# A four-layer metaformer on one core: the ranking's end reordered with rows from a root, and layer 1's normed rows on ScalarE

## The chip, the cores and the metric

The kernel runs on one core of a Trainium2 chip, in one launch. The metric is device time in microseconds (us), the median of several runs; a profile of one more execution shows what each engine did. The engines are TensorE (PE; its weight loads are shown as PEld), VectorE (DVE), ScalarE (ACT), GpSimd (POOL) and SyncE (SP), which here issues DMAs. Each engine works through its own queue in order.

## The reference

The input is an image batch x of shape (4, 64, 128, 128), fp32, seen as 256 matrices of 128 rows ("tokens") by 128 channels. Four layers follow one another, each with two residual halves: x + mixer(norm(x)), then x + ffn(norm(x)). The change lies in layer 1 (the second one):

```
# mixer of layer 1, per matrix (n = 128 rows)
score  = -(|q_i|^2 + |k_j|^2 - 2 q_i.k_j)        # 128 x 128, q = k = centred rows
ranks  = argsort(argsort(-score)) + 1            # place of each entry among all 128*128
weight = -log(ranks / (128*128));  weight /= sum over each row
x = x + dec(weight @ enc(norm(x)))
# ffn of layer 1
p, i = top_k(softmax(norm(x) @ router_w + router_b), 2);  p /= sum(p)
x = x + sum_k p_k * (norm(x) @ expert_w[i_k] + expert_b[i_k])      # 8 experts
```

Equal scores are ranked in order of their place in the matrix, since argsort is stable.

## The kernel before

The layers run one after another. Layer 1 is built of `l1_distances` (norm, products, the distances of all pairs), `l1_ranks` (the ranking) and `l1_blocks` (weights, values, experts).

**Ranking.** The 256 matrices are two groups of 128, one matrix on each partition. The distance matrix is symmetric, so only the upper triangle is sorted: 8128 pairs, padded to 8192 numbers per partition. `sort_stage` runs a merging network forward and stores which pairs were exchanged; `back_stage` runs it backwards on the places, so that `ranks[g]` holds each pair's rank, with flags for equal neighbours. Its end is `finish(g, ta, tb)`, called for group 0 and then for group 1:

- ScalarE copies the ranks to fp32 (L1546), VectorE finds the largest eight of each segment of 256 (L1550, L1551), which are the equal ones.
- VectorE masks the ranks (L1553), ScalarE spreads them into two halves of an int32 (L1556, two instructions), SyncE writes them to DRAM, one DMA for each of 127 rows of the triangle (L1560).
- The candidates are packed and up to 64 per partition picked (L1567 to L1584). Each is a place f in the triangle; its row is the number of row ends that are not above f: a comparison of 64 x 128 (L1591) and a sum (L1596). From row and column come two positions per equal pair, and a comparison of 128 x 128 (L1615) with a sum (L1620) tells how many come before each. TensorE turns the results (L1628), ScalarE keeps them in `ties` (L1629).

This part is ordered by a scheduler that works from the program's dependencies. A branch (L1835), at which all engines meet, chooses a slow path that is not taken with this input. Behind it come the constants of `l1_blocks` and its loads of the written ranks.

**Blocks.** `l1_blocks` handles eight matrices at a time, in 32 blocks. Each step is given to a planner (`Plan`) with its engine, an assumed time, what it reads and what it writes; the planner then fixes one order per engine over all blocks, in which several blocks overlap, so a change of a step's engine or assumed time can change the whole order. A block loads xt and the ranks (rt); GpSimd casts these to `above` and `below` (L2213). `normed` is run twice per block, ahead of the attention (k = "1") and ahead of the experts (k = "2"): statistics (`bn`, L1937), their merging (`merge`, L1943 to L1948), a first guess of 1/sqrt by ScalarE (L1952, L1953), its refinement (L1959 to L1963), then the normed rows: of every four, rows 0 and 2 by VectorE (L1979) and rows 1 and 3 by ScalarE (L1977). TensorE turns four of them (L1991, tile pt, two buffers) and ScalarE copies them out (L2003). Attention: `ta` and `tb` mark the equal pairs (L2013, L2014), TensorE adds the ranks up (L2018 to L2022), ScalarE takes the logarithm (L2027), values are made (L2032, L2038), weights times values (L2044), divided and added to x (L2052, L2055). Experts: logits (L2072, L2079), the top two and their shares (L2091 to L2125), turned (L2142) and copied (L2148); for each of eight experts TensorE spreads its share over the partitions (L2156, tile pr, two buffers), the rows are multiplied by it (L2166: five by VectorE, three by GpSimd from ScalarE's copy, L2162), TensorE adds up the products (L2183, L2185) and VectorE adds them to x (L2190). GpSimd stores xt (L2227).

## Time and profile before

| | us |
|---|---|
| runs | 11910.42, 11881.41, 11887.56 (median 11887.56) |
| profiled execution | 11887.27, its span 11885.4 |
| VectorE busy | 10015.2 (84% of the span) |
| ScalarE busy | 7406.1 (62%) |
| TensorE busy | 7219.7 (61%) |
| GpSimd busy | 6180.0 (52%) |
| first instruction behind the branch L1835 on VectorE | at 5277.49 |
| one block of the blocks' stage, L2142 to L2142 | 5838.96 to 5874.38 |

Starts are counted from the span's start. A row of the timeline gives start, duration, engine, line, operation, the tile written and those read, and in brackets the idle time of the engine before it with what ended it. Neighbouring instructions of one kind are merged (x4) and may overlap a little, so the distance between starts can be shorter than a duration. "SPq" is SyncE's queue of DMA issues.

### The profile page before, as it was taken

The numbers are of one execution on the slowest core, as the hardware profiler recorded it, in microseconds if no ns is written. First come the engines' busy times: TensorE is split into PE (matmuls) and PEld (weight loads), VectorE is DVE, ScalarE is ACT, GpSimd is POOL, SyncE is SP. The second block draws the span as 40 slices with busy tenths as digits, with TensorE's granted clock in tenths as the row PEclk, the third lists the DMA queues.
The fourth block names the chain that finished last, engine by engine and source line by source line (L and its number), as shares of the span: only waits on it lengthen the run. The fifth ranks groups of instructions, "written<-read, shape, count | busy, mean of one in ns | idle before, by whom it ended". The sixth has DMA issues, their size and how long they took to land. (4 is left out here: it accounts for less than half of the span.)

```text
span 11885.4 us, 113599 instructions
## 1 busy us (share of the span) xinstructions
PE 7219.7 (61%) x33966; PEld 4411.3 (37%) x33966; DVE 10015.2 (84%) x16358; ACT 7406.1 (62%) x10575; POOL 6180.0 (52%) x5274
## 2 busy tenths in 40 slices
PE   7877785000000000019997899989999999998665
PEld 5655553000000000018886344444444444446443
DVE  7567637999999999988996899999999999997454
ACT  4244534888867777623332787877878787875332
POOL 1000026999960000003232999988999999994222
PEclk8877797555555555559998999999999999999887
DMA  5312245111111111121111334333343433333434
GB/s 191 95 41 49 81 139 136 56 58 58 58 54 55 57 55 54 49 47 45 44 47 32 138 141 143 139 133 139 137 142 137 144 139 141 137 134 116 173 133 152
DMA packets 636713, 1193.45 MB, mean 100 GB/s; under 512 B 217036, under 2 KB 434478, under 8 KB 556974
## 3 DMA queue, kind: packets, MB, share of 16 engines
q1 hardware_dynamic: 592158, 1059.80, 26.6%
q0 software_dynamic: 34368, 124.14, 3.2%
q8 instruction: 273, 4.47, 0.2%
q10 hardware_dynamic: 9552, 2.08, 0.1%
q14 instruction: 362, 2.97, 0.1%
HBM read 950.89 MB, written 251.71 MB: 101 GB/s over the span
## 5 line engine op out<-in xcount | busy, mean ns | idle before, releaser
L2719 POOL TENSOR_TENSOR gs<-hist,cc 128x512 f32<-128x512 f32 x2048 | 2576.0, 1266 | 376.7 <-DVE hist L2714 232.1
L2714 DVE TENSOR_TENSOR_SCAN hist<-da,state,bs 128x512 f32<-128x512 f32 x1984 | 2521.7, 1271 | 0.0
L2728 PE MATMUL py<-gs,ident 128*128 128x512 f32 x4096 | 2241.5, 630 | 5.2 <-DVE y L2604 5.2
L1628 PE MATMUL pt<-ident,both 128*128 128x128 f32 x6 | 2.7, 447 | 3257.1 <-DMA pk<-spare 3185.5
L2685 ACT ACTIVATE da<-dt,am 128x512 f32<-128x512 f32 x2048 | 1414.6, 715 | 328.9 <-DVE hist L2714 326.6
L2706 DVE TENSOR_TENSOR bs<-dx,bs 128x512 f32<-128x512 f32 x2048 | 1391.3, 679 | 183.5 <-PE bs L2692 138.3
L1504 POOL TENSOR_TENSOR diff<-key 128x2048 f32<-128x2048 f32 (+11 forms) x364 | 1383.8, 3853 | 86.4 <-DVE key L1509 76.4
L1628 PEld LDWEIGHTS pt<-ident,both 128*128 128x128 f32 x6 | 1.1, 182 | 3258.6 <-issue 3258.6
L2728 PEld LDWEIGHTS py<-gs,ident 128*128 128x128 f32 x4096 | 738.0, 197 | 906.0 <-issue 437.3
L1886 POOL IOTA row<- 72x1 int32 x1 | 0.1, 137 | 1799.5 <-ACTq L1835 1799.5
L2692 PE MATMUL bs<-bt,pick 96*128 96x512 bf16 x2048 | 805.8, 394 | 144.5 <-DVE hist L2714 141.4
L1526 ACT COPY keep<-rank 128x1536 int16<-128x1536 int16 (+11 forms) x364 | 612.8, 1686 | 437.5 <-DVE rank L1528 388.6
L1502 ACT COPY low<-key 128x2048 f32<-128x2048 f32 (+11 forms) x364 | 627.4, 1724 | 284.1 <-DVE key L1509 275.7
L1527 DVE COPY_PREDICATED rank<-back,rank 128x1536 int16<-128x1536 uint8 (+11 forms) x364 | 781.4, 2147 | 16.7 <-ACT keep L1526 16.7
L1528 DVE COPY_PREDICATED rank<-back,keep 128x1536 int16<-128x1536 uint8 (+11 forms) x364 | 777.7, 2137 | 12.5
L1509 DVE TENSOR_TENSOR key<-low,key 128x2048 f32<-128x2048 f32 (+11 forms) x364 | 744.3, 2045 | 12.4
L1508 DVE TENSOR_TENSOR key<-low,key 128x2048 f32<-128x2048 f32 (+11 forms) x364 | 748.9, 2057 | 6.4 <-DMA key<-dist 3.9
L1505 ACT ACTIVATE turned<-diff 128x2048 int8<-128x2048 f32 (+11 forms) x364 | 600.2, 1697 | 36.6 <-DMA key<-dist 28.0
L1517 ACT ACTIVATE back<-turned 128x3072 uint8<-128x3072 int8 (+12 forms) x182 | 582.2, 3199 | 0.0
L2185 PE MATMUL pe<-ew,xg 128*128 128x128 f32 x4096 | 506.7, 277 | 0.0
L2185 PEld LDWEIGHTS pe<-ew,xg 128*128 128x128 f32 x4096 | 490.5, 194 | 4.0
L1026 POOL DMA_DIRECT2D state<-zz x16 | 18.5, 1157 | 855.2 <-DVE zz L1016 615.1
(825 smaller groups left out, 18223.0 us busy)
## 6 DMA issues: line engine op xcount, KB each, us to landing
cc<-cd SPq DMA_DIRECT2D x512, 1024.0 KB
xt<-state SPq DMA_DIRECT2D x64, 1024.0 KB
xo<-state SPq DMA_DIRECT2D x128, 256.0 KB
state<-xo POOLq DMA_DIRECT2D x128, 256.0 KB, 2.9
xl<-in_L_ffn_weight SPq DMA_DIRECT2D x32, 1024.0 KB
tk<-in_x SPq DMA_DIRECT2D x32, 512.0 KB
tokens<-tt POOLq DMA_DIRECT2D x32, 512.0 KB, 6.4
pk<-in_l1c_diag SPq DMA_DIRECT2D x32, 512.0 KB
```

The lines of the kernel that those rows point to most:

```text
L1504: nc.gpsimd.tensor_sub(d, lo[part], hi[part])
L1508: nc.vector.tensor_tensor(lo[part], c, hi[part], ALU.min)
L1509: nc.vector.tensor_tensor(hi[part], c, hi[part], ALU.max)
L1527: nc.vector.copy_predicated(l, t, h)
L1528: nc.vector.copy_predicated(h, t, kv)
L2185: T.matmul(w["pe"][:, j, :], w["xg"][:, q, j, :], ew[:, q, :], start=False, stop=(j == 3 and q == E - 1))
L2685: nc.scalar.activation(da, x_["dt%d" % b], AF.Exp, scale=am[:, s : s + 1])
L2692: nc.tensor.matmul(bs, pick[:, s, :], x_["bt%d" % b], start=True, stop=True)
L2706: nc.vector.tensor_mul(db, x_["dx%d" % b], db)
L2714: nc.vector.tensor_tensor_scan(h, live.pop(("da", t)), live.pop(("db", t)), 0.0 if first else state[b][:, s : s + 1], ALU.mult, ALU.add,)
L2719: nc.gpsimd.tensor_tensor(gs, h, live.pop(("cc", t)), ALU.mult)
L2728: nc.tensor.matmul(x_["py%d" % b], env.ident, live.pop(("gs", t)), start=(s == 0), stop=(s == S - 1))
```

## The change

Three things. (1) In `normed`, all eight rows are made by ScalarE, four in one step of an assumed 2.0 us; VectorE's steps of 0.7 and ScalarE's of 1.0 go. (2) In `merge`, the last small operation (variance times 1/C plus eps) is written with eps as a broadcast tensor in place of a scalar from a tile. (3) `finish` is split into `spread`, `candidates`, `equals`, `compare` and `lacking`, called in a new order for the two groups: both copies, group 0's spread, both searches, then the rest. The row of a place f comes from the quadratic's root, by Ln and Exp on ScalarE, and two corrections by at most one row; the comparison with all row ends, its sum and the table of row ends are gone.

```diff
-            nc.vector.tensor_tensor(
-                cmp, f.unsqueeze(2).to_broadcast([P, TIES, W]), rowend.unsqueeze(1).to_broadcast([P, TIES, W]),
-                ALU.is_ge,
-            )
-            nc.vector.tensor_reduce(row, cmp, AX.X, ALU.add)
...
+            nc.vector.tensor_scalar(x, f, -8.0, float((2 * W - 1) ** 2), ALU.mult, ALU.add)
+            nc.vector.tensor_scalar(x, x, 1.0, None, ALU.max)
+            nc.scalar.activation(x, x, AF.Ln)
+            nc.scalar.activation(x, x, AF.Exp, scale=0.5)
+            ri = sb.tile([P, TIES], I32, name="ri")
+            nc.vector.tensor_scalar(ri, x, -0.5, W - 0.5, ALU.mult, ALU.add)
+            nc.vector.tensor_copy(row, ri)
+            def start():
+                nc.vector.tensor_scalar(gap, row, -0.5, W - 0.5, ALU.mult, ALU.add)
+                nc.vector.tensor_mul(gap, gap, row)
+                nc.vector.tensor_sub(gap, f, gap)
+            start()
+            nc.vector.scalar_tensor_tensor(row, gap, 0.0, row, ALU.is_lt, ALU.subtract)
+            nc.vector.tensor_scalar(row, row, -1.0, None, ALU.mult)
+            start()
+            nc.vector.tensor_add(x, gap, row)
+            nc.vector.scalar_tensor_tensor(row, x, W - 1.0, row, ALU.is_ge, ALU.add)
+            start()
...
-        finish(0, keys[0], spare)
-        finish(1, keys[1], spare)
+        for g in range(2):
+            nc.scalar.copy(keys[g], ranks[g])
+        spread(0, spare)
+        found = [candidates(0, keys[0])]
+        found.append(candidates(1, keys[1]))
+        last = [equals(0, *found[0])]
+        before = [compare(last[0][3], keys[0])]
+        spread(1, keys[1])
+        last.append(equals(1, *found[1]))
+        lacking(0, *last[0][:3], before[0])
+        before.append(compare(last[1][3], keys[0]))
+        lacking(1, *last[1][:3], before[1])
...
-                V.tensor_scalar(mv[:, :, 1], mv[:, :, 1], 1.0 / C, eps, ALU.mult, ALU.add)
+                V.scalar_tensor_tensor(mv[:, :, 1], mv[:, :, 1], 1.0 / C, eps.to_broadcast([P, NB]), ALU.mult, ALU.add)
...
+            def affine(j0):
+                def f():
...
+                    for j in range(j0, j0 + 4):
+                        r, n = v["rs"][:, j : j + 1], v["nb"][:, j : j + 1]
+                        S.activation(v["xl"][:, j, :], v["xt"][:, j, :], AF.Identity, bias=n, scale=r)
...
-                    step("dve", 0.7, tags(0) + scales, "xl xl0 " + name, make, new="xl " + name)
+                    step("act", 2.0, tags(0) + scales, "xl xl0 " + name, affine(0), new="xl " + name)
                 else:
-                    step("dve", 0.7, tags(4) + scales + "xl", "xl4", affine((4, 6), V))
-                step("act", 1.0, tags(j0) + scales + "xl", "xm%d" % j0, affine((j0 + 1, j0 + 3), S))
+                    step("act", 2.0, tags(4) + scales + "xl", "xl4", affine(4))
```

`spread` holds the masking, ScalarE's two instructions and the 127 row writes of a group, `candidates` the search by segments, `equals` all from the packing to the positions, `compare` L1615 and `lacking` L1620 and what follows it. Group 1 is spread into `keys[1]`, which its search must have read by then; group 0 into `spare`.

## Prediction

> **What bounds the kernel now.** Views read in this order: the page's span and slices, the stretches of 250 us, the timeline of the ranking's end, SyncE's waits, one block of the blocks' stage engine by engine, and the order in which the two built programs queue their instructions. Only two stretches change order on any engine: the ranking's end (5082 to 5277 us) and layer 1's blocks (5290 to 6473 us). From the page:

> ```profile
> span 11885.4 us, 113599 instructions
> PE   7877785000000000019997899989999999998665
> DVE  7567637999999999988996899999999999997454
> ACT  4244534888867777623332787877878787875332
> ```

> Around slice 18 VectorE is full and TensorE idle; after it both stand at 9. The ranking's end, from its timeline:

> ```profile
> 5123.18 8.69 DVE L1591 TENSOR_TENSOR key<-f,rowend 128x8192 f32<-128x8192 f32 x1
> 5126.68 149.23 SPq L1560 DMA_DIRECT2D pk<-spare  x254
> 5131.99 8.68 DVE L1596 TENSOR_REDUCE row<-key 128x64 f32<-128x8192 f32 x1
> 5194.85 18.69 ACT L1556 ACTIVATE spare<-rank,base 128x8192 int16<-128x8192 int16 x2 [13.30 <-DVE rank L1553]
> 5241.84 17.22 DVE L1620 TENSOR_REDUCE rk<-key 128x128 f32<-128x16384 int16 x1
> 5263.95 0.14 POOL L1886 IOTA row<- 72x1 int32 x1 [1799.52 <-ACTq L1835]
> 5277.49 0.17 DVE L1870 MEMSET rw<- 128x128 f32 x1 [17.38 <-SPq L1835]
> ```

> The 254 row writes are two trains of 127 on SyncE: 5126.7 to 5187.2 (60.5 us) and 5213.6 to 5275.9 (62.3), each after ScalarE's pair of L1556. VectorE ends its last reduction at 5259.06; the branch L1835 lets everybody on at 5277.5, 1.6 us after SyncE's last write. So SyncE ends this stretch, and between its trains it waits for ScalarE, which waits for VectorE. One block:

> ```profile
> 5838.96 0.41 PE L2142 MATMUL pl<-identb,g 128*72 128x128 bf16 x4 [0.44 <-DVE g L2125]
> 5860.99 0.68 PE L1991 MATMUL pt<-ident,xl 128*128 128x128 f32 x4 [0.70 <-DVE xl L1979]
> 5862.23 0.71 PE L1991 MATMUL pt<-ident,xl 128*128 128x128 f32 x4 [0.56 <-DVE xl L1979]
> 5874.38 0.41 PE L2142 MATMUL pl<-identb,g 128*72 128x128 bf16 x4 [0.43 <-DVE g L2125]
> 5851.81 0.53 DVE L1943 TENSOR_TENSOR d<-st 128x8 f32<-128x8 f32 x1
> 5853.60 1.18 DVE L1948 TENSOR_SCALAR mv<-mv,eps 128x8 f32<-128x8 f32 x1
> 5859.77 2.92 DVE L1979 TENSOR_SCALAR xl<-xt,rs,nb 128x128 f32<-128x128 f32 x4
> 5851.28 1.04 POOL L2213 CAST below<-rt 128x1024 f32<-128x1024 int16 x1
> 5853.49 1.27 POOL L2166 TENSOR_TENSOR xg<-xT,gr 128x512 f32<-128x512 f32 x1 [1.17 <-ACT gr L2162]
> 5859.50 2.59 POOL L2166 TENSOR_TENSOR xg<-xT,gr 128x512 f32<-128x512 f32 x2 [4.74 <-ACT gr L2162]
> ```

> Columns: start, duration, engine, line, operation, and in brackets the idle time before and what ended it. A block takes 35.42 us (L2142 to L2142). Pitch is the distance from start to start where nothing waits. TensorE's pitches sum to 31.75: eight L2185 groups of 1.80, four L1991 and two L2072 of 0.89, two L2032 of 0.90, four L2044 of 0.45, two runs L2018 to L2022 of 1.98, 16 L2156 of 0.22, and 0.96 for L2142 and L2183. It loses 0.59 for g (L2142), 0.49 for v and 0.73 for copies in the middle, and 0.87 + 0.79 + 0.10 for normed rows: 3.6. VectorE and GpSimd block each other: L1948 lasts 0.23 alone and 1.18 until GpSimd's product ends; four rows of L1979 last 1.1 alone and 2.9 beside two products.

> **Ranking's end, removed and moved.** L1591 and L1596 go for both groups: 2 x (8.69 + 8.68) = 34.7 us of VectorE. The masking and ScalarE's spread of group 0 come first. ScalarE copies both ranks (7.02 each) until 5089.7, then spreads until 5108.4 (18.7); train 0 starts there, 18.3 us earlier, and ends at 5168.9. Group 1's spread needs its candidates read: 5082.6 + 2.3 (mask) + 2 x 23.05 (64 pairs of MAX8 and index) = 5131.0, the mask to 5134, ScalarE to 5152.8: before train 0 ends. Train 1 follows without a gap: 5168.9 + 62.3 = 5231.2, with the branch 5232.8. Both trains keep their 127 issues each at about 0.48 us; behind them on SyncE stand only the branch and the constants' loads, which come earlier with them.

> **Added on VectorE.** After 5131.0: heads, 16 MAX8 and 14 replacements of both groups interleaved and the second mask, 18.5 (by the rows of group 1 alone and the interleaved ones), to 5149.5. Then it waits for the roots: ScalarE's Ln and Exp stand behind group 1's spread, 5152.8 + 4 x 0.2, so to 5153.7: a new wait of 4.2, and all the compares are queued behind it. Were a table load (L1955's row is 1.28) needed for each function it would be 2.6 more; L1952 and L1953 run Ln and Exp without one. Then 41 small operations, interleaved, 0.135 each (independent neighbours start 0.10 apart, dependent ones 0.23): 5.5. Four L1615/L1620 of 17.2 and their tails: 70.3, last reduction ending at 5229.5. Engines stood at the branch 4.9 after it (5259.06 to 5263.95): 5234.4. VectorE, not SyncE, is then last, by 1.6. The stretch gives 5277.5 - 5234.4 = **43 us** (39 with table loads and slow small operations, 45 if only SyncE counts). The lost rowend load is at nothing: it lay at the sort's start.

> **Blocks, what goes.** Eight L1979 per block: 1.18 + 2.84 = 4.0 us of VectorE's pitch. ScalarE gets eight rows more, 0.42 each (1.65 for four): 3.4 on an engine at 34%. L1948 becomes an operation with a tensor for eps. Its nearest rows: L1946, 0.15 alone; L1943, which like it reads two tensors of SBUF, 0.17 alone and 0.53 beside GpSimd's cast, until that ends. So it goes on waiting beside L2166, gain 0 to 1.0; either is hidden, since the next product (L2166 at 5854.78) waits for TensorE's spread of 5854.36 anyway. I take 0. [...]

> **Blocks, the new order.** It repeats every two blocks. I followed it with the rows above. First block: as before for 17 us. ScalarE then does two blocks' four rows from 5856.2 to 5859.45, the copy for L2162 moves from 5858.8 to 5859.4; the turn at 5859.7 does not wait. Losses left: 0.49 + 0.73 as before, 0.19 for the second four rows, 0.12 for xT behind them, 0.43 for g: 2.0. Second block: g is ready, and VectorE does L2190 (0.60), L2052/L2055 (0.73), L2038 (0.60), four L1937 (0.79) and eight L2013/L2014 (1.54) before the first L2166 that frees a "pr" buffer (0.69): 4.95, where TensorE has 3.4 to do: 1.5 lost. The last three L2013/L2014 now lie beside a GpSimd product; early in the stage these operations met casts:

> ```profile
> 5297.70 1.07 DVE L2014 TENSOR_SCALAR tb<-placeb,ties 128x128 bf16<-128x128 bf16 x1
> 5297.69 1.04 POOL L2213 CAST below<-rt 128x1024 f32<-128x1024 int16 x1
> ```

> That costs 1.3 more. Five spreads in a row over two buffers lose 1.5, xT2's copy behind another block's four rows 1.0, g 0.5: 5.8. A pair: 2 x 31.75 + 7.8 = 71.3 against 70.84. Over 12 such pairs **+5.5 us**; without the collision 70.0, so -10; with a second collision in each +20. L1991's wait thus goes, and late next is "pr", behind VectorE's queue.

> **Blocks, the start.** From the first statistics to the fifth block's L2142 the trace has 58.6 + 23.8 + 40.2 + 35.3 + 35.4 = 193.3 us, for 145 us of TensorE's pitches. The new order holds the same work, but runs three blocks' attention together between the third and fourth block: counting its rows at their pitches (TensorE / VectorE) the intervals hold 36.6/46.5, 13.4/12.2, 22.3/21.1, 57.9/47.9, 15.1/18.0. With the overheads seen (17, 7.7, 3.2 to 3.7 per interval) and 10 for the long one: 64 + 19 + 26 + 69 + 22 = 200. **+8 us**, -10 to +25 (the granted clock was at 0.5 until 5365 in this part; more gaps could keep it there).

> Sum: -43 + 5.5 + 8 = -29.5. The profiled execution took 11887.27 (1.9 beside its span), the median is 11887.56: **11858 us**. Alone its range is 11840 to 11880.

> **Rivals.** (1) L1991's 1.76 us per block simply go and "pr" does not bite: 28 x 1.76 = 49 less, 11887 - 43 - 49 + 8 = 11803. For it: VectorE falls to 28 us of pitches against TensorE's 31.75. Against: the queue order above. Chance 0.25. (2) Slower: the bf16 L2013/L2014, four sets of eight per pair, each meet GpSimd, one operation passing per product, in series with the first L2166. At 1.2 us per meeting it passes break-even at 30 / 12 / 1.2, or two to three meetings more than my one; at six more per pair 86 us: 11858 + 86 = 11944. For it: 1.03 and 1.07 above. Against: two of the sets fall where GpSimd is idle and one where VectorE waits anyway. 0.06. (3) The ranking's end stays: if the trains back to back ran at half pace, SyncE would end at 5108 + 246 = 5354, later than now; at the same pace it can't. DMA share was 0.40 at most in a train, so no: 0.04 for losing half the gain, 11880. Mine has 0.65.

> **Numbers.** 0.3% (35.7 us, about what a measurement of this kernel can tell from no change) is 11852. Of mine a third lies below that, two thirds within: faster 0.22 + 0.25 = 0.47, same 0.43 + 0.04 = 0.47, slower 0.06. The range runs from the middle of rival 1 to the end of mine and a little over: 11806 to 11886.

> **What would show it.** Right: L1835 lets go near 5234; one train of 254 without gap from 5108; waits of L1597 on ScalarE about 4; pairs of L2142 about 71.3 apart over two blocks, TensorE waiting at L2156 for VectorE's L2166; the blocks no shorter than 1183 us. Wrong: a gap in the trains, table loads between Ln and Exp, a pair under 69 us, L1977's successors waiting for ScalarE's other copies for long, or a clock of 0.5 past the sixth block.

## The result, and the profile after

The changed kernel takes 11886.60 us (median of 20 runs, 11867.78 to 11901.63), the kernel before 11889.39 us in 20 runs beside it: a ratio of 0.9996, 95% interval 0.9989 to 1.0002. That is no change that can be measured. The forecast was 11858 us, 29.5 below a kernel before of 11887.56; 2.8 below that is 11884.8, at the upper end of the range of 11806 to 11886. The profiled execution took 11901.63 us, 14 us more than that of before; of this 6 us lie ahead of the ranking's end and 17 us behind the blocks, in code that the change doesn't touch and whose order is the same. So the stages are compared by themselves, each from its own first mark.

From the page of the changed kernel, the rows that answer to those of before (40 slices of the span, tenths of busy time):

```profile
span 11899.9 us, 113703 instructions
...
PE   7877785000000000029997899999999999998665
...
DVE  7567637999999999987885999999999999996454
ACT  4244534888867777633443787877877787775332
```

In slices 18 to 21, counted from 0, VectorE (DVE) stands at 7885 instead of 8996, and in 19 to 21 ScalarE (ACT) at 443 instead of 332, as rows on ScalarE must give. TensorE (PE) is as full as it was, 9997. The ranking's end, from the changed kernel's timeline (start, duration, engine, line, operation, and in brackets the idle time before and what ended it):

```profile
5095.65 18.66 ACT L1545 ACTIVATE spare<-rank,base 128x8192 int16<-128x8192 int16 x2
5139.88 18.68 ACT L1545 ACTIVATE key<-rank,base 128x8192 int16<-128x8192 int16 x2 [25.57 <-DVE rank L1542]
5158.44 0.37 ACT L1594 ACTIVATE x<-x 128x64 f32<-128x64 f32 x2
5158.72 0.38 ACT L1595 ACTIVATE x<-x 128x64 f32<-128x64 f32 x2
...
5114.38 60.91 SPq L1549 DMA_DIRECT2D pk<-spare  x127
5175.38 60.34 SPq L1549 DMA_DIRECT2D pk<-key  x127
...
5158.99 0.34 DVE L1597 TENSOR_SCALAR ri<-x 128x64 int32<-128x64 f32 x2 [2.93 <-ACT x L1595]
...
5216.60 17.22 DVE L1643 TENSOR_REDUCE rk<-key 128x128 f32<-128x16384 int16 x1
...
5240.29 0.17 DVE L1903 MEMSET rw<- 128x128 f32 x1 [4.51 <-ACTq L1868]
```

The second train of 127 writes begins 0.1 us after the end of the first (5114.38 + 60.91 = 5175.29). Ln (L1594) and Exp (L1595) run straight behind the spread, with no table load between, and VectorE waits 2.93 us for them. SyncE ends at 5235.7, VectorE's last reduction at 5233.8 with a tail of small copies behind it. From the last copy of the ranking's backward pass to the branch the kernel before takes 204.4 us (5073.1 to 5277.5), the changed one 161.1 (5079.2 to 5240.3): 43.3 us less, and 43 were forecast.

So the blocks took it back. One place of their steady order, which comes once in each pair of blocks:

```profile
5718.07 0.71 PE L2071 MATMUL po<-v,wT 128*128 128x129 f32 x4
5718.72 0.38 PE L2183 MATMUL pr<-gb,pick 72*128 72x512 bf16 x1
5720.96 0.38 PE L2183 MATMUL pr<-gb,pick 72*128 72x512 bf16 x1 [1.87 <-DVE xg L2193]
5721.56 0.38 PE L2183 MATMUL pr<-gb,pick 72*128 72x512 bf16 x1 [0.22 <-DVE xg L2193]
5722.16 1.09 PE L2183 MATMUL pr<-gb,pick 72*128 72x512 bf16 x2 [0.22 <-DVE xg L2193]
5723.05 1.13 PE L2071 MATMUL po<-v,wT 128*128 128x129 f32 x4
...
5739.35 1.16 PE L2099 MATMUL pl<-rw,xT 128*128 128x128 f32 x8 [0.72 <-ACT xT L2030]
...
5718.82 1.27 DVE L2040 TENSOR_SCALAR ta<-placeb,ties 128x128 bf16<-128x128 bf16 x1
5720.23 1.87 DVE L2193 TENSOR_TENSOR xg<-xT,pr 128x512 f32<-128x512 f32 x3
...
5718.75 1.29 POOL L2193 TENSOR_TENSOR xg<-xT,gr 128x512 f32<-128x512 f32 x1 [0.74 <-ACT gr L2189]
```

TensorE waits 1.87 us for the product that frees a buffer of pr. VectorE is late with it because the masks ta and tb stand ahead of it and the last ta meets GpSimd's (POOL's) product, that is, runs beside it and ends only with it: 1.27 us, where it takes 0.25 alone. All that was forecast. What was not: behind 5722.65, where a clock record of 0.5 begins, the same group of four L2071 takes 1.13 us instead of 0.71. The windows from one L2169 group to the next show why. Columns: length, busy time (and instructions) of PE, PEld, DVE, ACT and POOL, then the clock granted to TensorE, the DMA share and GB/s:

```profile
5606.10:5642.50 36.40, 35.50 (x293) 32.28 (x294) 30.60 (x103) 14.94 (x35) 10.77 (x12) 1.00 0.15 44
5642.50:5678.70 36.20, 32.38 (x244) 27.41 (x244) 28.18 (x95) 14.85 (x35) 10.67 (x10) 0.95 0.15 45
5678.70:5715.10 36.40, 35.48 (x292) 32.26 (x292) 30.58 (x103) 14.94 (x35) 10.76 (x12) 1.00 0.15 44
5715.10:5751.10 36.00, 32.22 (x245) 27.66 (x246) 28.97 (x95) 14.84 (x35) 10.73 (x10) 0.95 0.16 45
5787.40:5824.70 37.30, 33.65 (x245) 28.64 (x245) 27.48 (x95) 14.84 (x35) 10.71 (x10) 0.91 0.15 43
```

Before the change the granted clock is 1.00 throughout from the fifth block to the 31st. Now every second block has 0.95 or 0.91: by the clock records of the trace one or two periods of 3.41 us at 0.5. The stage in parts, by first L2142 (L2169 in the changed kernel) of each block, in us, and the time at a granted clock of 0.5 in one of them; the other columns are experiments that are told below:

| part | before | changed | ranking only | rows, old order | old rows, new order | fill_more |
|---|---|---|---|---|---|---|
| branch to first block | 70.5 | 71.8 | 68.5 | 69.4 | 75.3 | 71.4 |
| first to fifth block | 135.6 | 142.6 | 135.6 | 135.6 | 148.1 | 145.9 |
| fifth to seventh | 70.9 | 77.6 | 70.9 | 69.4 | 83.7 | 77.0 |
| seventh to 31st | 851.1 | 871.9 | 850.7 | 834.6 | 935.7 | 852.8 |
| 31st to the stage's end | 108.0 | 106.3 | 107.7 | 107.3 | 106.2 | 104.9 |
| whole stage | 1236.0 | 1270.2 | 1233.4 | 1216.4 | 1349.1 | 1251.9 |
| half clock, seventh to 31st | 0 | 51.2 | 0 | 0 | 95.6 | 0 |

The stage is 34.2 us longer; 13.5 were forecast.

### The profile page after: what moved, and what is told of

Read it like the earlier page. It is cut to its first block, busy times and chain, and to the rows that moved or that the text cites. A ratio compares the mean times of both kernels' runs of the same rounds, so it can differ in the third digit from the quotient of the medians.

```text
span 11899.9 us, 113703 instructions
## 1 busy us (share of the span) xinstructions
PE 7274.6 (61%) x33966; PEld 4444.6 (37%) x33966; DVE 9889.4 (83%) x16124; ACT 7499.5 (63%) x10835; POOL 6177.7 (52%) x5274
## 5 line engine op out<-in xcount | busy, mean ns | idle before, releaser
L1502 ACT ACTIVATE turned<-diff 128x2048 int8<-128x2048 f32 (+11 forms) x364 | 600.6, 1700 | 36.6 <-DMA key<-dist 27.7
L1026 POOL DMA_DIRECT2D state<-zz x16 | 18.5, 1156 | 857.2 <-DVE zz L1016 619.5
```

## The experiments

Theory A: the ranking's end gives its 43 us, and the blocks take them back by the order that the planner writes out from the new steps. Rivals: the work behind the branch takes the gain back by itself; rows on ScalarE are late whatever the order.

**The ranking alone.** The kernel before with the change's `spread`, `candidates`, `equals`, `compare` and `lacking`, and the old blocks.

> The kernel before with the change's new end of the ranking alone; the blocks' stage is the old one. Theory A (the ranking's end gives what was forecast and the blocks take it back by the order that the planner writes out): the branch lets go near 5234, the blocks' stage from branch to its end stays at 1236 us, and the time falls by about 43 us, to a ratio of 0.9964. Rival (the work behind the branch gives the gain back by itself, as its loads and constants come earlier): branch near 5234 all the same, blocks' stage 1250 or more, time less than 25 us lower.

Measured: 11834.99 us, ratio 0.9952 (0.9938 to 0.9965). The stretch up to the branch takes 161.4 us, the blocks' stage 1233.4. Theory A holds: nothing behind the branch takes it back. (The medians differ by 58 us, and these two stretches show 45.6 of them; the rest lies in stages that are the same and stays unexplained.)

**Rows on ScalarE in the old order.** The planner sees the old steps, so every engine's order of steps stays; only what two steps issue differs.

```diff
-                affine((0, 2), V)()
...
-                    step("dve", 0.7, tags(4) + scales + "xl", "xl4", affine((4, 6), V))
-                step("act", 1.0, tags(j0) + scales + "xl", "xm%d" % j0, affine((j0 + 1, j0 + 3), S))
+                    step("dve", 0.7, tags(4) + scales + "xl", "xl4", lambda: None)
+                step("act", 1.0, tags(j0) + scales + "xl", "xm%d" % j0, affine(range(j0, j0 + 4), S))
```

> The new end of the ranking, and in the blocks all eight normed rows on ScalarE, but every engine's order of steps as before the change (the planner sees the old steps; the old VectorE step issues nothing, ScalarE's step does four rows; eps as before). Theory A: TensorE's wait for the normed rows, 1.76 us per block, falls to 0.4 to 0.8, the granted clock stays at 1.0, the blocks' stage takes 1197 to 1211 us, the time falls by 43 + 25 to 39, to about 11818. Rival B (rows on ScalarE are late by themselves, whatever the order): TensorE waits for ScalarE's rows 1.7 us per block or more, the stage takes 1236 us or more.

Measured: 11822.00 us, ratio 0.9942 (0.9928 to 0.9955), the fastest version here: its five runs (11804.97 to 11828.77) all lie below the five of the ranking alone (11831.42 to 11850.16). The stage takes 1216.4 us: 17.0 less than with the ranking alone, where 22 to 36 had been expected. Waits of TensorE in 19 blocks (engine, tile, line, for whom: us, times, longest), first of the kernel with the ranking alone, then of this one:

```profile
PE pt L2024 <- DVE xl L2012: 23.9, 38, 0.7
PE pl L2175 <- DVE g L2158: 8.4, 19, 0.5
```

```profile
PE pl L2171 <- DVE g L2154: 8.8, 20, 0.5
PE pl L2101 <- ACT xT L2032: 8.8, 19, 0.5
PE pr L2185 <- ACT gr L2191: 5.0, 18, 0.3
```

The wait for the normed rows goes whole (1.26 us per block). In its place comes one for xT, 0.46 per block: ScalarE's copy (L2032) now stands behind four more rows. A block takes 34.7 us instead of 35.4. So rows on ScalarE are a gain, if the order stays.

**The new order with the old rows.** The reverse: the changed kernel's plan, but in the step of four rows VectorE makes rows 0 and 2.

```diff
                     for j in range(j0, j0 + 4):
                         r, n = v["rs"][:, j : j + 1], v["nb"][:, j : j + 1]
-                        S.activation(v["xl"][:, j, :], v["xt"][:, j, :], AF.Identity, bias=n, scale=r)
+                        if j % 2:
+                            S.activation(v["xl"][:, j, :], v["xt"][:, j, :], AF.Identity, bias=n, scale=r)
+                        else:
+                            V.tensor_scalar(v["xl"][:, j, :], v["xt"][:, j, :], r, n, ALU.mult, ALU.add)
```

> The new end of the ranking, and in the blocks the order of the changed kernel with the engines of the old one: inside the step of four rows, VectorE makes rows 0 and 2, ScalarE 1 and 3 (eps as before). Theory A: the order costs what was lost, and VectorE's 4 us per block stand in its queue ahead of the buffers that TensorE waits for: a pair of blocks takes 73 to 77 us, the clock falls to 0.5 in each pair, the stage takes 1280 to 1330 us, the time is 5 to 50 us above that of the kernel before. Rival B (rows on ScalarE cause the loss): the stage is back at 1236 to 1245 us without a fall of the clock, the time falls by 35 to 43 us.

Measured: 11962.28 us, ratio 1.0061 (1.0047 to 1.0075); the stage takes 1349.1 us, 19 more than the expected upper end, a pair of blocks 78.4. The four stages with the new ranking make a square: with old rows the new order costs 1349.1 - 1233.4 = 116 us, with rows on ScalarE 1270.2 - 1216.4 = 54 us; moving the rows gains 17 us in the old order and 79 in the new. (The changed kernel differs from its corner by the eps operation too, and the next run shows that at nothing, in the old order.) It is the order that loses, and moving the rows hides about half of that loss.

**Eps alone.** Only the operation with variance and eps.

> The kernel before with the tensor operation for variance and eps alone. Forecast: no difference (within 6 us); the operation goes on lasting until GpSimd's product ends, about 1.2 us where they meet. Rival (the operation passes GpSimd, 0.2 us instead of 1.2 once per block): VectorE earlier by 1 us per block and the time 10 to 30 us lower.

Measured: ratio 0.9995 (0.9986 to 1.0004). Its line in 21 blocks, before and in this run (duration in ns, least, median, greatest):

```profile
L1948 DVE TENSOR_SCALAR mv<-mv,eps x42: 230/705/1189, 5603.8 to 6314.5; 128x8 f32<-128x8 f32 x42
```

```profile
L1948 DVE SCALAR_TENSOR_TENSOR mv<-mv,eps x42: 167/698/1245, 5607.9 to 6318.5; 128x8 f32<-128x8 f32 x42
```

Alone it is 0.06 us shorter, beside GpSimd as long as it was. The two medians stand between one meeting and one free run per block.

**TensorE kept busy in its wait.** The trace showed the clock's fall behind the wait for pr. This run gives TensorE something to do there and changes no order.

```diff
+                    if seen[0].endswith("gpssgos"):
+                        pv = ps1.tile([P, 4, C], F32, name="pv")
+                        for _ in range(8):
+                            T.matmul(pv, identb, pick4, start=True, stop=True)
                     w["pr", q] = ps2.tile([P, 4, P], F32, name="pr")
```

(`seen` collects a letter for each step that TensorE is given, so that the place is found.)

> The changed kernel with eight matmuls of 128x512 (0.22 us each at full clock) put into TensorE's queue once per pair of blocks, at the place where it waits 1.9 us for VectorE's product that frees a buffer of pr; their result is read by nobody. Theory C (the clock falls to 0.5 because TensorE is idle there, and that costs 2.0 of the 72.9 us of a pair): the clock stays at 1.0, a pair takes 70.5 to 71.5 us although TensorE has more to do, the blocks' stage falls by 15 to 28 us, the time to 11858 to 11872. Rival D (the fall of the clock comes with something else, or costs nothing since VectorE sets the pace): the pair stays at 72.9 us or grows by up to 1.8, the time at 11887 or more.

Measured: 11866.67 us, ratio 0.9992 (0.9983 to 1.0002): not separable from the kernel before by itself. The profile tells more. The half clock between the seventh and 31st block falls from 51.2 to 20.5 us, that part from 871.9 to 861.2; the whole stage takes 1263.0 us, 7 less where 15 to 28 were expected: the clock still falls in some pairs, and the part from the first to the fifth block takes 3 us more. Two blocks of one kind in this run:

```profile
5709.50:5744.20 34.70, 32.56 (x252) 27.48 (x252) 28.28 (x95) 14.84 (x35) 10.74 (x10) 1.00 0.16 47
5780.60:5817.00 36.40, 34.25 (x253) 28.53 (x254) 27.45 (x95) 14.85 (x35) 10.67 (x10) 0.95 0.15 44
```

Their waits are the same, to 0.02 us each. One has a period of half clock, the other not, and it costs 36.4 - 34.7 = 1.7 us, half of 3.41. So theory C holds for the price. The trace also shows that the eight matmuls stand in nine of the eleven pairs that had the fall; in the last two the letters come in another order, and TensorE waits 1.84 us as before. Three of the six periods of half clock left lie behind those two waits. The other three come in pairs whose long wait is filled, where only short waits and sparse work are left.

**More of the same.** Two matmuls more behind each of the next three spreads.

```diff
-                    if seen[0].endswith("gpssgos"):
+                    more = {"gpssgos": 8, "pssgoss": 2, "ssgosss": 2, "sgossss": 2}.get(seen[0][-7:], 0)
+                    if more:
                         pv = ps1.tile([P, 4, C], F32, name="pv")
-                        for _ in range(8):
+                        for _ in range(more):
```

> The kernel of the fill run with two more such matmuls (0.22 us each) behind each of the next three spreads of the group, where TensorE otherwise does 0.22 us of work in every 0.6 us. With eight matmuls alone the clock still fell, for one period of 3.4 us, in some of the pairs whose waits were the same as in the others. Theory G (what counts is how much TensorE does in a period, short waits and sparse work included): no period of half clock between the seventh and the 31st block, every pair at 71.1 to 71.6 us, the blocks' stage 1250 to 1262 us. Rival H (the periods are set off by something other than TensorE's load, or the extra matmuls delay the spreads by as much as they save): periods of half clock in two or more of the pairs, or pairs of 72 us and more.

Measured: 11859.15 us, ratio 0.9982 (0.9970 to 0.9995). No period of half clock from the seventh block to the 31st, pairs of 71.1 us (two of 71.5, and the last of 69.5, as in the changed kernel), the stage 1251.9 us. Two blocks of the kind that had the falls:

```profile
5714.80:5749.60 34.80, 33.21 (x258) 28.21 (x260) 28.35 (x95) 14.86 (x35) 10.83 (x10) 1.00 0.16 46
5785.90:5820.70 34.80, 33.17 (x258) 28.12 (x259) 28.36 (x95) 14.85 (x35) 10.83 (x10) 1.00 0.16 46
```

Theory G holds, and the last two pairs say more than was planned: there the wait stays open, 1.85 us, and only five extra matmuls stand behind it, and yet the clock does not fall. So a wait of that length need not lower it; the sparse work behind it counts too. Work that nobody reads makes this part shorter than in the changed kernel: 871.9 - 852.8 = 19.1 us, 0.8 us per block. The two kernels were not timed side by side; their ratios to the kernel before, 0.9982 and 0.9996, differ by 17 us, which fits. And the steady order at full clock takes 71.1 us per pair, where 71.3 had been forecast.

**The masks behind the first two products.** The step that makes TensorE late, moved on VectorE.

```diff
+            def tied():
+                if seen[0].endswith("gps"):
+                    kept.append(masks)
+                else:
+                    masks()
...
+                    if eng is V and kept and q >= 2:
+                        kept.pop()()
```

> The changed kernel with one step moved on VectorE, once per pair: the four ta and four tb that stand between the statistics and the first product of the new group come behind its first two products. Theory C (VectorE's queue ahead of the product makes TensorE wait, and the wait lowers the clock): VectorE's first product starts 2.3 to 2.8 us earlier, the wait of 1.9 us at pr goes or falls under 0.5, the clock stays at 1.0, a pair takes 69 to 70.8 us instead of 72.9, the time is 11838 to 11862. Rival D (another thing is late at the same place, as ScalarE's copy of gb or the masks' reader): the pair falls by less than 1 us, the time by less than 12.

Measured: 11890.27 us, ratio 1.0009 (1.0000 to 1.0018); a pair takes 74.1 us, 1.1 more than the 73.0 of the changed kernel. A miss. The first product does come earlier, but the waits move:

```profile
5792.87 0.38 PE L2198 MATMUL pr<-gb,pick 72*128 72x512 bf16 x1 [0.56 <-DVE xg L2209]
5793.97 0.38 PE L2198 MATMUL pr<-gb,pick 72*128 72x512 bf16 x1 [0.73 <-ACT gr L2204]
5796.19 0.38 PE L2198 MATMUL pr<-gb,pick 72*128 72x512 bf16 x1 [1.84 <-DVE xg L2209]
...
5794.06 1.25 DVE L2042 TENSOR_SCALAR ta<-placeb,ties 128x128 bf16<-128x128 bf16 x1
```

The masks now stand between the second product and the third, and the last ta meets GpSimd's next product again, 1.25 us. In this stretch VectorE has too much to do for two buffers of pr; where the masks stand in it decides only which spread waits. The next runs test that reading.

**One pair of masks out of four.** Theory E: it is these masks that VectorE has too much. Run in the changed kernel and, as a control, with the old blocks.

```diff
-                for j in range(4):
+                for j in range(1):
                     col, row, lack = (ties[:, k, v["i"] + j0 + j : v["i"] + j0 + j + 1] for k in range(3))
...
-                    T.matmul(w["pt"][:, j, :], w["ta"][:, j, :], w["tb"][:, j, :], start=False, stop=(j == 3))
+                    T.matmul(w["pt"][:, j, :], w["ta"][:, 0, :], w["tb"][:, 0, :], start=False, stop=(j == 3))
```

> The changed kernel with one of every four pairs of masks ta and tb made (six instructions of eight left out, 1.2 us of VectorE per set; TensorE uses the one pair four times, so equal ranks are not told apart rightly). Theory E (the masks, the last of them lying beside GpSimd's product, are what VectorE has too much ahead of and among the products in the stretch after the second turn of the gates): TensorE's waits at pr for VectorE fall from 24 us in ten pairs to under 8, the clock stays at 1.0, a pair takes 69.3 to 70.6 us. Rival F (any queue there would do it: the products themselves are too slow for two buffers, masks or none): the waits stay over 15 us and the pair over 72.

> The same six masks of eight left out in the kernel with the new end of the ranking and the old blocks. A control: there TensorE waits for VectorE's normed rows and not at pr. By theory E a pair falls by less than 1 us, from 70.96 to above 69.9, since the rows meet GpSimd's products as before; by the rival that VectorE's sum of work sets the pace everywhere it falls by 2 us or more.

Measured: in the new order 11831.03 us, ratio 0.9961 (0.9947 to 0.9975); a pair takes 70.0 us instead of 73.0. The waits at pr for VectorE in 728 us, about ten pairs, of the changed kernel and of this run (us, times, longest; under 8 had been expected):

```profile
PE pr L2183 <- DVE xg L2193: 24.2, 38, 1.9
```

```profile
PE pr L2183 <- DVE xg L2193: 8.5, 22, 0.6
```

In the old order, one run, a pair takes 70.96 us with and without these masks. So the same VectorE work costs 3 us per pair in one order and nothing in the other. About 1 of the 3 goes through the clock: the pairs at full clock take 69.1 here and 71.1 in the run with more filling. The clock did not stay at 1.0, as had been expected: it fell in every second pair.

```profile
5541.90:5574.60 32.70, 30.48 (x244) 26.62 (x244) 25.09 (x83) 14.73 (x35) 10.63 (x10) 1.00 0.17 49
5611.00:5645.40 34.40, 32.17 (x244) 27.71 (x244) 24.25 (x83) 14.73 (x35) 10.63 (x10) 0.95 0.16 47
```

```profile
5614.60 0.59 PE L2183 MATMUL pr<-gb,pick 72*128 72x512 bf16 x2
5615.76 0.38 PE L2183 MATMUL pr<-gb,pick 72*128 72x512 bf16 x1 [0.56 <-DVE xg L2193]
5616.36 0.88 PE L2183 MATMUL pr<-gb,pick 72*128 72x512 bf16 x2 [0.22 <-DVE xg L2193]
5617.17 0.68 PE L2071 MATMUL po<-v,wT 128*128 128x129 f32 x4
5617.97 0.79 PE L2183 MATMUL pr<-gb,pick 72*128 72x512 bf16 x2
5618.55 1.91 PE L2045 MATMUL pt<-below,ident 128*128 128x512 f32 x2
```

In this place the longest wait is 0.56 us, and the clock falls at 5618.23 all the same (L2045 takes 1.91 us; in the block without a fall 1.02).

**The halves of the ranking's change.** The root in the old sequence, and the new sequence with the old comparison and sum for the rows (L1591 and L1596 of before, in `keys[0]`).

> The kernel before with the rows from the root, but the ranking's end called as before: group 0 from its search to its end, then group 1, both spread into the same tile. Theory A (both halves of the change are needed): group 1's mask on VectorE comes 10 to 15 us earlier, SyncE's second train starts after a gap of 10 to 16 us, the branch lets go at 5260 to 5268 instead of 5277 to 5282, 12 to 17 us of the 43. Rival (the root gives nearly all): branch before 5245.

> The kernel before with the ranking's end in the new sequence, each group spread into a tile of its own, but rows by comparison with all row ends and a sum. Theory A: the two trains stand back to back and end near 5234, but VectorE ends 25 us later than in the changed kernel (34.7 for the two comparisons and sums, less 9 for the small operations and the wait for the roots), so the branch lets go at 5255 to 5263, about 18 us of the 43. Rival (the sequence alone gives it all, SyncE being last): branch before 5245.

Measured, in one run each, from the last copy of the backward pass to the branch, against 204.4 us before and 161.1 with both: 201.8 with the root alone, 188.3 with the sequence alone. The root alone, 2.6 us, missed its forecast of 12 to 17. In its trace the first train runs from 5118.5 to about 5179, and ScalarE spreads group 1 only after that:

```profile
5184.22 0.26 ACT L1594 ACTIVATE x<-x 128x64 f32<-128x64 f32 x1 [19.35 <-DVE x L1593]
5184.50 0.26 ACT L1595 ACTIVATE x<-x 128x64 f32<-128x64 f32 x1
5184.80 18.70 ACT L1545 ACTIVATE spare<-rank,base 128x8192 int16<-128x8192 int16 x2
```

In ScalarE's queue the spread stands behind group 1's Ln and Exp, which wait for VectorE until 5184.2; and as both groups are spread into the same tile, `spare`, it could not have overwritten that before about 5179, the first train's end. So an earlier VectorE is of little use there. The sequence alone gives 16.1 us (18 expected). Its two trains stand back to back (127 issues from 5115.83, 127 from 5176.43), and VectorE's last reduction, ending at 5264.0, is last. The branch at 5268.9 lies outside the 5255 to 5263 expected since that execution was 7.5 us late before this stretch. Both halves together give 43.3, more than twice the sum of the halves: each half takes away the bound that hides the other.

## Why the prediction was right or wrong

The time lies at the end of the range, but the sum that led there did not come out: of 29.5 us forecast as a gain 2.8 were measured. The ranking's end gave what was forecast; the blocks took back far more, by a term that the sum did not have.

**The ranking's end, -43: right.** 43.3 in the changed kernel, 43.0 in the run with it alone (161.4 us). The trains without a gap, no table load, VectorE's wait for the roots (2.93 us against 4.2) and both engines ending within a few us of each other were as forecast.

**The start of the blocks, +8: right in the sum, partly by luck.** From the first statistics to the fifth block 192.9 us before and 201.4 after: 8.5. The five intervals were forecast at 64, 19, 26, 69 and 22 us and measure 58.8, 23.9, 26.8, 71.3 and 20.6: misses of 5 us either way that cancel.

**Eps, 0: right**, shown by the run of it alone.

**The steady order, +5.5: the step that failed.** The place, the wait and its cause were as written: VectorE's queue ahead of the first product, the masks in a meeting of 1.27 us, xT2's copy 0.7 late (forecast 1.0). The sum of it holds too: 71.3 us per pair forecast, 71.1 when TensorE is kept at full clock. But the sum took TensorE's pitches at a granted clock of 1.0, and the new order has a stretch in which TensorE waits and does little; each period of 3.41 us that is granted at 0.5 for it costs time that the sum put at nothing: pairs with one take 72.2 to 72.8 us and pairs with two 73.6 to 73.9, against 71.1 with none in the filled kernels. So the stage from the seventh block to the 31st is 20.8 us longer in place of 5.5 (19.1 of them go when the clock is kept at 1.0), and between the fifth and the seventh, which the forecast counted as steady, another 6.7, with 13.7 us at half clock against none before. There the extra runs did not part the order from the clock (77.0 us with 10.2 at half clock in the last filled run). The forecast named a clock of 0.5 past the sixth block as a sign of being wrong, gave that a price only for the stage's start, and no row of its sum allowed for it later.

**Rival 1 (the waits for the rows simply go, 0.25): wrong for this change**, right in direction for another one. In the old order the wait does go, and 17 us come of it, not 49: by the rows of waits it was 1.26 us per block, and 0.46 of a new wait for xT come in its place.

**Rival 2 (masks meeting GpSimd, 0.06): not the case in that number**, but its mechanism is what the masks show: whether they cost nothing or 3 us per pair depends on where they stand. **Rival 3 (the trains at half pace): wrong.** 60.91 and 60.34 us.

**The total.** Forecast -43 + 5.5 + 8 = -29.5. The profile has -43.3 + 34.2 = -9.1 in these stages; the medians differ by -2.8, and how much of the rest is run-to-run change of the untouched stages is left open.

## What to carry to other kernels

A plan that is computed from assumed costs can turn into another order when one step changes its engine; try the same move with the old order held fixed before you judge it, as here the move gained 17 us and the order lost 54. When a sum of pitches says that the busiest engine stays busy, look for the stretch where it does least, since the clock, which fell behind such a stretch here, charged for it a second time (1.7 us for a period of 3.41 us at 0.5 in the first filled run). Two edits that lift different bounds of one stretch can be worth little alone, as here 2.6 and 16.1 us against 43.3 with both; cost them together.

## What the runs showed of the hardware

An estimate from the traces, counting every matmul at its pitch at full clock (0.22 us for a spread, 0.11 for one of 128x128 in fp32, 0.43 for one of L2045): from the seventh block to the 31st of the changed kernel the period ahead of a fall held 19 to 39% of a period's work, and every other period at full clock 55% or more. In the run with fewer masks, by the rows printed with it, the period ahead of 5618.23 held 46%; 21 periods earlier, over the same waits in a pair without a fall, the one from 5546.55 held 66%. So by this estimate the two pairs differ in how the same gaps lie on the grid. No sharp line shows: in the kernel before, periods of 48% passed without a fall (from 5717.2, for one), and ahead of the fifth block of the changed kernel one of 37% did (from 5405.2), while one of 39% (from 5480.3) came before a fall. The share that decides is left open.
